# A two-layer graph, state-space and LSTM kernel: first loads, a pool over the set-up's memory, and the place of the recurrence's weight preparation

## The chip, the cores and the metric

The kernel runs on one core of a Trainium2 chip. The metric is device time in microseconds (us) of one execution. The engines are named as the profile names them: PE (matrix multiply, with PEld for its weight loads), DVE (vector), ACT (scalar and activation functions), POOL (GpSimd), SP (the engine that issues most DMAs; its instruction queue is SPq).

## The reference, cut to what matters

The input is x of shape (32, 512, 256) and an integer adjacency adj of shape (32, 512, 512). The 32 entries of the first axis are called elements here. Two layers follow each other, each with a residual connection around each of its two halves:

```python
x = x + L0_gnn(layernorm(x), adj, ...)   # per-element graph attention with edge types, 4 heads
x = x + L0_ffn(layernorm(x), ...)        # per-element Mamba-2 block, 512 tokens in chunks
x = x + L1_gnn(layernorm(x), adj, ...)   # per-element graph attention, one head
x = x + L1_ffn(layernorm(x), ...)        # LSTM over the 512 tokens, all 32 elements at once
```

The first three steps work on one element at a time. The fourth is an LSTM of 512 dependent time steps whose batch is the 32 elements. It needs all elements of the third step before its first time step. Its weights (`wih`, `whh`, the biases, `wl`, `bl`, `fw`, `bw`) are used there alone.

## The kernel before, in words

`layers_per_batch` does the first three steps for all elements and writes the result to the DRAM tensor `X3`; `recurrence` does the LSTM from `X3`. A second copy of `layers_per_batch` in a conditional block stands for adjacencies of other values and is not taken in these runs.

**Set-up (lines 105 to 247).** Constants are made, then some twenty weights are loaded through SP's queue in the order in which the lines stand: `w0`, `w0t`, `asrc`, `adst`, three rows, `win` (1160 KB), and so on to `a1`. Weights that only the set-up uses (`w0t`, `asrc`, `adst`, `normw`, `woutt`, `wlin`, `w1t`, `a1`) lie in the pool `wset`. PE multiplies some of them together (L154, L166, L243), DVE copies the results out (L205, L212, L247). Then `setup.close()` (L249) gives the memory of `wset` back, and the pools `io`, `one` and `two`, opened after it, may take it. `io` holds the element inputs: `adj` (1024 KB, one buffer) and `x` (512 KB, four buffers).

**One element.** `plain0` (L470) loads `adj` and `x` (L474, L476), normalises x, makes a transposed 8-bit adjacency, and computes the attention of layer 0. `after0` (L315) adds it to x after a normalisation per head, with POOL for the reciprocal root (L54, L56) and for the last products and sums (L336, L337). `mamba_in` (L582) normalises again and transposes (xm, mT), `mamba_dt` (L593) makes step sizes and decays, `mamba` (L665) does the rest in 25 steps; the first thing in it that the profile shows on ACT is the Silu of L680, and POOL does `ce` (L729), `xdd` (L776) and the gating of `xh` (L800) in it. `plain1` (L910) is the attention of layer 1, and `after1` (L853) stores the element to `X3` (L862). Mamba's tiles `csr`, `ce`, `bT`, `cT` and `ssr` have one buffer each, in the pool `one`.

**What sets the order of the work.** The parts of all elements are written as Python generators that are merged by a hand-made clock (L988 to L1001): `mamba` of element b runs from b to b+1, `plain0` of element b+2 from b+0.86 to b+1.54, `after0` from b+1.65 to b+1.76, `plain1` of element b-1 from b+0.571 to b+0.86. This gives the program order. From it the framework fixes, at build time, one order of instructions for each engine: an instruction goes in front of others that stand ahead of it in the program if its inputs are ready earlier by the framework's own time estimates. Each engine then works through its order and waits at each instruction for its inputs. `recurrence` has a hand-written order instead (L1255).

**The recurrence's weights.** `recurrence_weights` (L1030) is one more generator, which brings the LSTM's weights into another order and scale and stores them to the DRAM tensor `wr`. Its place on the clock is 3.25 plus 0.375 for each step (L996). It begins with a head: `wl`, `bl` and two biases are loaded and combined, then `fw` and `bw` are loaded, halved and stored. Then come 16 items, 8 of `wih` and 8 of `whh`. An item loads raw columns (L1099 and L1101, or four loads at L1105), subtracts (L1108), reorders and scales with a memset and four products into the tile `rwt` (L1051, L1057), and stores `rwt` to `wr` (L1116). `rwt` has one buffer, so the memset of the next item waits until the store of the item before has landed. The rows stored are 128, but 127 (`r = P - 1`, L1115) for the last four items of `wih`. In the trace all of this stands between 17.7 and about 159 us: none of its inputs depend on anything, so it was put in front of what stands ahead of it in the program. `recurrence` loads `wr` at L1259.

Of the kernel before, what the change touches and what calls it, by code (L numbers as in the profile page):

```python
# [19 lines left out]
P = 128  # L20
N = 512
# [54 lines left out]
def layers_per_batch(ctx, tc, c, a, X3, odd=None, wr=None):  # L76
# [22 lines left out]
    def load_row(src, name):  # L99
        t = wp.tile([P, src.shape[1]], F32, name=name)  # L100
        nc.sync.dma_start(out=t, in_=src.to_broadcast([P, src.shape[1]]))
        return t


    tri = wp.tile([P, P], F32, name="tri")
    late = wp.tile([P, P], F32, name="late")
# [14 lines left out]

    setup = ExitStack()
    wset = setup.enter_context(tc.tile_pool(name="wset", bufs=1))
    w0 = load_k(a.w0, D, "w0")
    w0t = load_k(a.w0t, D, "w0t", wset)
    asrc = load_k(a.asrc, T0, "asrc", wset)
    adst = load_k(a.adst, T0, "adst", wset)
    bias0 = load_row(a.bias0, "bias0")
    gamma = load_row(a.gamma, "gamma")
    beta = load_row(a.beta, "beta")  # L130
    win = load_k(a.win, DIN, "win")
    convw = load_k(a.convw, 4, "convw")
    convb = load_k(a.convb, 1, "convb")
    dtb = wp.tile([NH, 1], F32, name="dtb")
    nc.sync.dma_start(out=dtb, in_=a.dtb.rearrange("o h -> h o"))
    alog = load_row(a.alog, "alog")
    dcol = load_k(a.dcol, 1, "dcol")
    normw = load_k(a.normw, 1, "normw", wset)
    woutt = load_k(a.woutt, DI, "woutt", wset)
    wlin = load_k(a.wlin, D, "wlin", wset)  # L140
    blin = load_row(a.blin, "blin")
    w1 = load_k(a.w1, D, "w1")
    w1t = load_k(a.w1t, D, "w1t", wset)
    a1 = load_k(a.a1, 2, "a1", wset)

    def score_weights0(vec, half, name):

# [99 lines left out]
        nc.vector.tensor_scalar(wc[:, cc, :], pw[:, :D], normw[:, cc, :], None, ALU.mult)  # L247

    setup.close()  # L249
    io = ctx.enter_context(tc.tile_pool(name="io", bufs=2))  # L250
    one = ctx.enter_context(tc.tile_pool(name="one", bufs=1))
    two = ctx.enter_context(tc.tile_pool(name="two", bufs=2))

# [86 lines left out]
    def attention0(b, state):  # L340


        adj = io.tile([P, NT, N], I32, tag="adj", bufs=1, name=f"adj{b}")
        nc.sync.dma_start(out=adj, in_=a.adj[b].rearrange("(i p) j -> p i j", p=P))
        x = io.tile([P, NT, D], F32, tag="x", bufs=4, name=f"x{b}")
        nc.sync.dma_start(out=x, in_=a.x[b].rearrange("(i p) d -> p i d", p=P))
        xn = two.tile([P, NT, D], F32, tag="rowa", name=f"xn{b}")
        layernorm(nc, small, c, xn, x, NT)
        nc.gpsimd.tensor_tensor(x, x, beta.unsqueeze(1).to_broadcast([P, NT, D]), ALU.add)
# [120 lines left out]
    def plain0(b, state):  # L470


        adj = io.tile([P, NT, N], I32, tag="adj", bufs=1, name=f"adj{b}")
        nc.sync.dma_start(out=adj, in_=a.adj[b].rearrange("(i p) j -> p i j", p=P))  # L474
        x = io.tile([P, NT, D], F32, tag="x", bufs=4, name=f"x{b}")
        nc.sync.dma_start(out=x, in_=a.x[b].rearrange("(i p) d -> p i d", p=P))  # L476
        xn = two.tile([P, NT, D], F32, tag="rowa", name=f"xn{b}")
        layernorm(nc, small, c, xn, x, NT)
        nc.gpsimd.tensor_tensor(x, x, beta.unsqueeze(1).to_broadcast([P, NT, D]), ALU.add)
# [113 lines left out]
    def mamba_dt(b, state):  # L593

        mT = state["mT"]

        csr = one.tile([P, N], F32, tag="csr", name=f"csr{b}")
        dtr = csr[64 : 64 + NH, :]
        pd = bank(f"pdt{b}")
        for k in range(DK):  # L600
            nc.tensor.matmul(pd[:NH], win[:, k, DIN - NH :], mT[:, k, :], start=(k == 0), stop=(k == DK - 1))
        nc.scalar.activation(dtr, pd[:NH], AF.Identity, bias=dtb)

        def columns(rows, at, name):

            pt = bank(f"p{name}")
            for i in range(NT):
                nc.tensor.transpose(pt[:, i * NH : (i + 1) * NH], rows[:, i * P : (i + 1) * P], at)
            t = small.tile([P, NT, NH], F32, tag=name[:3], name=name)
            nc.vector.tensor_copy(t.rearrange("p i h -> p (i h)"), pt[:, : NT * NH])  # L610
            return t

        raw = columns(dtr, c.ident[64 : 64 + NH, 64 : 64 + NH], f"raw{b}")
        yield


        ee = small.tile([P, NT, NH], F32, tag="ee", name=f"ee{b}")
        nc.vector.scalar_tensor_tensor(ee, raw, -1.0, raw, ALU.mult, ALU.min)
        nc.scalar.activation(ee, ee, AF.Exp)
        u = small.tile([P, NT, NH], F32, tag="u", name=f"u{b}")  # L620
        nc.vector.tensor_scalar(u, ee, 2.0, None, ALU.add)
        nc.vector.reciprocal(u, u)
        nc.vector.tensor_tensor(u, u, ee, ALU.mult)
        u2 = small.tile([P, NT, NH], F32, tag="u2", name=f"u2{b}")
        nc.vector.tensor_tensor(u2, u, u, ALU.mult)
        q = small.tile([P, NT, NH], F32, tag="q", name=f"q{b}")
        nc.vector.tensor_scalar(q, u2, 2.0 / 17, None, ALU.mult)
        for m in (15, 13, 11, 9, 7, 5, 3):
            nc.vector.scalar_tensor_tensor(q, q, 2.0 / m, u2, ALU.add, ALU.mult)
        nc.vector.scalar_tensor_tensor(q, q, 2.0, u, ALU.add, ALU.mult)  # L630
        dt = small.tile([P, NT, NH], F32, tag="dt", name=f"dt{b}")
        nc.vector.scalar_tensor_tensor(dt, raw, 0.0, q, ALU.max, ALU.add)
        nc.vector.tensor_tensor(da[:, :, :NH], dt, aneg.unsqueeze(1).to_broadcast([P, NT, NH]), ALU.mult)
        yield


        pcs = bank(f"pcs{b}")
        for i in range(NT):
            nc.tensor.matmul(pcs[:32, i * P : (i + 1) * P], da[:, i, :], tri, start=True, stop=True)
        nc.scalar.copy(csr[:NH, :], pcs[:NH])  # L640
        nc.scalar.activation(csr[32 : 32 + NH, :], pcs[:NH], AF.Exp)
        line = way.tile([1, 2 * NH * N], F32, tag="line", name=f"line{b}")
        for n in range(2):
            nc.scalar.dma_start(
                out=line[:, n * NH * N : (n + 1) * NH * N].rearrange("o (h l) -> (o h) l", h=NH),
                in_=csr[32 * n : 32 * n + NH, :],
            )
        cs = columns(csr[:NH, :], c.ident[:NH, :NH], f"cs_{b}")
        pdc = bank(f"pdc{b}")
        nc.tensor.matmul(pdc[:, : NT * NH], late, da[:, :, :NH], start=True, stop=True)  # L650
        nc.tensor.matmul(pdc[:, NT * NH : 2 * NT * NH], ones, da[:, :, :NH], start=True, stop=True)
        dec = small.tile([P, 2, NT, NH], F32, tag="dec", name=f"dec{b}")
        nc.scalar.activation(dec.rearrange("p a i h -> p (a i h)"), pdc[:, : 2 * NT * NH], AF.Exp)
        yield

        ce = one.tile([P, NC, N - P], F32, tag="ce", name=f"ce{b}")
        for k in range(2):
            nc.sync.dma_start(
                out=ce[k * DS : (k + 1) * DS],
                in_=line[:, NH * N :].rearrange("o (c two l) -> o c two l", two=2, l=N)[:, :, k, P:].to_broadcast([DS, NC, N - P]),  # L660
            )
        state.update(dt=dt, cs=cs, dec=dec, ce=ce, line=line)
        yield

    def mamba(b, state):  # L665
# [14 lines left out]
            nc.scalar.activation(zs[:, cc, :], pz, AF.Silu)  # L680
            yield
        xh = two.tile([P, NC, N], F32, tag="wide", bufs=4 if odd is not None else 3, name=f"xh{b}")
        bT = one.tile([DS, N], F32, tag="bT", name=f"bT{b}")
        cT = one.tile([P, N], F32, tag="cT", name=f"cT{b}")
        def convolved(cc):
            pz = channels(DI + cc * P, f"px{b}_{cc}")
            acc = two.tile([P, N], F32, tag="acc", name=f"acc{b}_{cc}")
# [147 lines left out]
        pss = bank(f"pss{b}")  # L835
        for cc in range(NC):
            nc.tensor.matmul(pss[32 * cc : 32 * (cc + 1), :], ones[:, :32], zs[:, cc, :], start=True, stop=True)
        ssr = one.tile([P, N], F32, tag="ssr", name=f"ssr{b}")
        nc.scalar.copy(ssr, pss)
        pst = bank(f"psc{b}")  # L840
        for i in range(NT):
# [151 lines left out]
    ]  # L993
    if odd is not None:
        rw = ctx.enter_context(tc.tile_pool(name="rw0", bufs=1))
        streams.append(3.25 + (nb - 8) / 64 * n for n, _ in enumerate(recurrence_weights(nc, rw, a, wr)))  # L996
    END = nb + 10
    at = [next(t) for t in streams]
    while min(at) < END:
# [27 lines left out]
        nc.vector.tensor_scalar(odd, pf[:1, :1], P - 0.5, None, ALU.is_lt)  # L1027


def recurrence_weights(nc, pool, a, wr):  # L1030

# [15 lines left out]
    def ordered(raw, n, s):  # L1049
# [7 lines left out]
            nc.gpsimd.tensor_scalar(dst, src, half[g] * s, None, ALU.mult)  # L1057
        return t


    wl = tile_(P, 2 * DK, "rwl")
    for q in range(Q):
        for l in range(2):
            nc.sync.dma_start(
# [2 lines left out]
            )  # L1067
    yield
    nc.gpsimd.tensor_tensor(wl[:, :DK], wl[:, DK:], wl[:, :DK], ALU.subtract)
    bl = tile_(P, 2, "rbl")  # L1070
    nc.sync.dma_start(out=bl, in_=a.bl.to_broadcast([P, 2]))
    b = [tile_(P, 4 * J, f"rwraw{n}") for n in range(2)]
    for t, src in zip(b, (a.bih, a.bhh)):
        nc.sync.dma_start(out=t[:Q], in_=src.rearrange("o (q r) -> (o q) r", q=Q))
    yield
# [6 lines left out]
    nc.sync.dma_start(out=last, in_=t[:Q])  # L1082
    yield
    for n, src in enumerate((a.fw, a.bw)):
        t = tile_(P, W, "rwt")
        for q in range(Q):
            nc.sync.dma_start(out=t[q * GB : (q + 1) * GB, :J], in_=src[q : q + 1, :].to_broadcast([GB, J]))
        yield
        nc.gpsimd.tensor_scalar(t[:, :J], t[:, :J], 0.5, None, ALU.mult)
        yield  # L1090
        nc.sync.dma_start(out=wr[:, n0 + n * J : n0 + (n + 1) * J], in_=t[:, :J])
        yield
    for n, (src, s) in enumerate(((a.wih, 1.0), (a.whh, 0.5))):
        for k in range(DK):
            for q in range(Q):
                raw = tile_(P, 4 * J, f"rwraw{q % 2}")
                cols = slice(q * 4 * J, (q + 1) * 4 * J)
                if n == 0:
                    nc.sync.dma_start(out=raw, in_=src[k * P : (k + 1) * P, cols])  # L1099
                    off = tile_(P, 4 * J, "rwoff")  # L1100
                    nc.sync.dma_start(out=off, in_=src[D - 1 : D, cols].to_broadcast([P, 4 * J]))  # L1101
                else:
                    for r in range(Q):
# [352 lines left out]
```

## Time and profile before

| What | us |
|---|---|
| median of 3 runs (lowest, highest) | 4697.27 (4695.42, 4697.93) |
| the profiled execution's own time | 4702.24 |
| its span, first to last instruction | 4700.4 |
| first `adj` load issued (L474) | 29.9 |
| first Silu of `mamba`, element 0 (L680) | 146.3 |
| store of element 0 and of element 31 to `X3` issued (L862) | 334.9 and 3380.2 |
| first load of the recurrence issued (L1161) | 3386.4 |
| busy: PE, DVE, ACT, POOL | 3892.5, 3388.8, 2926.4, 1332.6 |

A row of the timeline gives the start and length of a group of instructions in us, the engine, the line of the kernel, the operation with the tile that it writes and those that it reads, their shape, the number of instructions, and in brackets how long the engine had been idle before it and what ended that. A row of the waits gives the waiting engine, tile and line, what it waited for, and total us, times and longest us. POOL's busy time ends in the 29th of the 40 slices of the page: the recurrence hardly uses it.

### The profile page before, as it was taken

What the parts mean: (1) busy time and instruction counts of PE and PEld (TensorE: products, weight loads), DVE (VectorE), ACT (ScalarE), POOL (GpSimd) and SP (SyncE); (2) the same over time, 40 slices, a digit from 0 to 9 for tenths busy, and PEclk for the clock granted to TensorE, in tenths of its full rate; (3) what the DMA queues carried; (4) which work ended last, traced back from release to release, by engine and by line L of the source; (5) the groups of instructions that cost most, each with busy time, mean ns of one, the idle gap of its engine ahead of it and who ended that gap; (6) DMA issues with size and microseconds to landing.
All of it is one profiled execution on the core that took longest, in us unless ns stands there. A gap on an engine that the chain in (4) does not pass through costs nothing. (4 is left out here: it accounts for less than half of the span.)

```text
span 4700.4 us, 115757 instructions
## 1 busy us (share of the span) xinstructions
PE 3892.5 (83%) x46798; PEld 2418.6 (51%) x46798; DVE 3388.8 (72%) x10205; ACT 2926.4 (62%) x6724; POOL 1332.6 (28%) x1148
## 2 busy tenths in 40 slices
PE   3788888888888888888888888888688888888883
PEld 2344444444444544444444444444466666666662
DVE  3466676666666666666666676666489999999997
ACT  2577777777777777776677776766444444444442
POOL 3433333433333433333433333432100000000000
PEclk7899999999999999999999999999799999999997
DMA  4222111222111222111122211211212222222225
GB/s 114 60 64 71 59 59 57 64 73 71 59 59 57 64 73 71 59 59 57 58 70 70 64 62 57 63 51 50 63 35 44 44 44 46 46 47 44 44 42 164
DMA packets 273754, 288.69 MB, mean 61 GB/s; under 512 B 151872, under 2 KB 224536, under 8 KB 271032
## 3 DMA queue, kind: packets, MB, share of 16 engines
q1 hardware_dynamic: 269832, 271.32, 20.3%
q10 hardware_dynamic: 3216, 9.81, 0.7%
q8 instruction: 372, 6.09, 0.5%
q14 instruction: 174, 1.43, 0.1%
q0 software_dynamic: 160, 0.04, 0.0%
HBM read 227.09 MB, written 37.11 MB: 56 GB/s over the span
## 5 line engine op out<-in xcount | busy, mean ns | idle before, releaser
L1243 PE MATMUL pg<-wall,h 128*32 128x96 f32 x16352 | 559.2, 277 | 176.7 <-DVE h L1325 169.3
L1243 PEld LDWEIGHTS pg<-wall,h 128*32 128x32 f32 x16352 | 374.8, 109 | 350.3 <-DVE h L1325 331.8
L1243 PE MATMUL pg<-wall,xTr 128*32 128x96 f32 (+1 forms) x16384 | 549.0, 274 | 0.0
L467 DVE SCALAR_TENSOR_TENSOR w<-w,adjT 128x1024 f32<-128x1024 f32 x256 | 348.1, 1380 | 247.6 <-ACT w L461 247.6
L1243 PEld LDWEIGHTS pg<-wall,xTr 128*32 128x32 f32 x16384 | 447.7, 110 | 4.9 <-issue 0.3
L743 ACT ACTIVATE g<-bc,cs 128x128 f32<-128x128 f32 x1024 | 321.9, 391 | 137.3 <-PE py L811 137.3
L1302 ACT ACTIVATE z<-pg 128x96 f32<-128x96 f32 x512 | 128.7, 251 | 439.3 <-PE pg L1243 439.3
L693 DVE SCALAR_TENSOR_TENSOR acc<-px,convw,acc 128x511 f32<-128x511 f32 (+2 forms) x480 | 347.2, 745 | 75.8 <-ACT acc L688 68.0
L461 ACT ACTIVATE w<-rb,neg,colsa 128x512 f32<-128x512 f32 x512 | 387.4, 806 | 9.9 <-DMA rb<-linea 6.0
L729 POOL TENSOR_TENSOR ce<-ce,cT 128x384 f32<-128x384 f32 x128 | 185.2, 1477 | 667.7 <-ACT cT L701 650.5
L533 PE MATMUL pav<-w,hb 128*64 128x512 f32 x1024 | 352.5, 615 | 22.5 <-DVE w L467 22.5
L830 PE MATMUL po<-wc,xh 128*128 128x256 f32 x1024 | 283.4, 422 | 100.2 <-POOL xh L800 100.2
L1313 ACT ACTIVATE z<-z 128x32 f32<-128x32 f32 x1024 | 234.7, 229 | 168.0 <-DVE z L1311 100.8
L945 PE MATMUL pov<-wb,wv 128*128 128x257 f32 x1024 | 243.1, 390 | 89.3 <-DVE wv L467 89.3
L54 POOL TENSOR_SCALAR ve<-mv 128x4 f32<-128x4 f32 x32 | 6.2, 195 | 1064.1 <-DVE mv L1167 1064.1
L672 PE MATMUL px<-mT,win 128*128 128x512 f32 x640 | 305.2, 607 | 0.0
L830 PEld LDWEIGHTS po<-wc,xh 128*128 128x128 f32 x1024 | 203.2, 213 | 145.3 <-POOL xh L800 115.6
L945 PEld LDWEIGHTS pov<-wb,wv 128*128 128x128 f32 x1024 | 191.5, 192 | 133.1 <-DVE wv L467 105.3
L56 POOL TENSOR_TENSOR rs<-ve,mhalf 128x4 f32<-128x4 f32 (+1 forms) x192 | 255.2, 1329 | 15.9
L800 POOL TENSOR_TENSOR xh<-xh,zs 128x512 f32<-128x512 f32 x128 | 175.5, 1381 | 282.1 <-DVE xh L799 282.1
L1325 DVE STREAM_TRANSPOSE h<-hh 128x32 f32<-128x32 f32 x1024 | 216.7, 212 | 34.9
L672 PE MATMUL pz<-mT,win 128*128 128x512 f32 x512 | 240.4, 602 | 0.0
(243 smaller groups left out, 8492.0 us busy)
## 6 DMA issues: line engine op xcount, KB each, us to landing
bc<-line SPq DMA_DIRECT2D x128, 512.0 KB
adj<-in_adj_dram SPq DMA_DIRECT2D x32, 1024.0 KB
rb<-linea SPq DMA_DIRECT2D x64, 512.0 KB
ce<-line SPq DMA_DIRECT2D x64, 384.0 KB
x<-in_x_dram SPq DMA_DIRECT2D x32, 512.0 KB
X<-x SPq DMA_DIRECT2D x32, 512.0 KB
xt<-X SPq DMA_DIRECT2D x128, 128.0 KB
x<-X SPq DMA_DIRECT2D x128, 128.0 KB
```

The source lines that it names most:

```text
L56: nc.gpsimd.tensor_tensor(rs, ve, c.mhalf[:, :n], ALU.pow)
L461: nc.scalar.activation(w[:, t, k, :], rb[:, k, :], AF.Relu, bias=neg1, scale=cols[:, 2 * m + t, h + k : h + k + 1],)
L467: nc.vector.scalar_tensor_tensor(w[:, :, k, :], w[:, :, k, :], 1.0, edges, ALU.add, ALU.mult)
L533: nc.tensor.matmul(pa[k * HO : (k + 1) * HO, :], hb[:, j, 2 * q + k, :], w[:, t, k, :], start=(j == 0), stop=(j == NT - 1),)
L672: nc.tensor.matmul(pz, win[:, k, col : col + P], mT[:, k, :], start=(k == 0), stop=(k == DK - 1))
L693: nc.vector.scalar_tensor_tensor(acc[:, s:], pz[:, : N - s], convw[:, cc, k : k + 1], acc[:, s:], ALU.mult, ALU.add)
L743: nc.scalar.activation(g[:, i, k, :], bc[:, k, i * P : (i + 1) * P], AF.Relu, bias=cs[:, i, 2 * cc + k : 2 * cc + k + 1], scale=-1.0,)
L830: nc.tensor.matmul(po[:, i * D : (i + 1) * D], xh[:, cc, it * P : (it + 1) * P], wc[:, cc, :], start=(cc == 0), stop=(cc == NC - 1),)
L945: nc.tensor.matmul(po[:, : D + 1], ws[j // 2][:, j % 2, 0, it * P : (it + 1) * P], wb[:, j, :], start=(j == 0), stop=(j == NT - 1),)
L1243: nc.tensor.matmul(p[q * GB : (q + 1) * GB, :], lhs[k], w[:, k, q, s:e], start=(start and k == 0), stop=(stop and k == DK - 1),)
L1313: nc.scalar.activation(z[:, (10 + n) * H : (11 + n) * H], z2[:, 4 * n * H : (4 * n + 1) * H], AF.Tanh, scale=0.5)
L1325: nc.vector.transpose(h[n], half)
```

## The change

Four things are changed. (1) The pool `io` is opened ahead of the set-up, element 0's `x` is loaded ahead of everything else, and its `adj` after `w0t`, `asrc`, `adst` and `w0`; the other set-up loads are put in another order. For later elements `x` is now loaded ahead of `adj`. (2) A new pool `mam` is opened after `setup.close()` and holds `csr`, `ce`, `bT`, `cT` and `ssr`, one buffer each, in the memory that `wset` gave back. (3) `recurrence_weights` is placed at `nb - 1.75` plus 1.5/64 for each step, that is from 30.25 on. (4) Each tile that it loads from DRAM is first written in one column by a POOL copy from x of the element that the clock has reached (`begun`), so that the loads can't be issued ahead of that x.

```diff
+    io = ctx.enter_context(tc.tile_pool(name="io", bufs=2))
+
+    def load_x(b):
+        x = io.tile([P, NT, D], F32, tag="x", bufs=4, name=f"x{b}")
+        nc.sync.dma_start(out=x, in_=a.x[b].rearrange("(i p) d -> p i d", p=P))
+        return x
+
+    def load_adj(b):
+        adj = io.tile([P, NT, N], I32, tag="adj", bufs=1, name=f"adj{b}")
+        nc.sync.dma_start(out=adj, in_=a.adj[b].rearrange("(i p) j -> p i j", p=P))
+        return adj
+
+    x0 = load_x(0)
...
-    w0 = load_k(a.w0, D, "w0")
     w0t = load_k(a.w0t, D, "w0t", wset)
     asrc = load_k(a.asrc, T0, "asrc", wset)
     adst = load_k(a.adst, T0, "adst", wset)
+    w0 = load_k(a.w0, D, "w0")
+    adj0 = load_adj(0)
+    beta = load_row(a.beta, "beta")
     bias0 = load_row(a.bias0, "bias0")
     gamma = load_row(a.gamma, "gamma")
-    beta = load_row(a.beta, "beta")
+    alog = load_row(a.alog, "alog")
+    blin = load_row(a.blin, "blin")
     win = load_k(a.win, DIN, "win")
...
-    alog = load_row(a.alog, "alog")
     dcol = load_k(a.dcol, 1, "dcol")
+    w1t = load_k(a.w1t, D, "w1t", wset)
+    a1 = load_k(a.a1, 2, "a1", wset)
+    w1 = load_k(a.w1, D, "w1")
     normw = load_k(a.normw, 1, "normw", wset)
     woutt = load_k(a.woutt, DI, "woutt", wset)
     wlin = load_k(a.wlin, D, "wlin", wset)
-    blin = load_row(a.blin, "blin")
-    w1 = load_k(a.w1, D, "w1")
-    w1t = load_k(a.w1t, D, "w1t", wset)
-    a1 = load_k(a.a1, 2, "a1", wset)
...
     setup.close()
-    io = ctx.enter_context(tc.tile_pool(name="io", bufs=2))
+
+    mam = ctx.enter_context(tc.tile_pool(name="mam", bufs=1))
     one = ctx.enter_context(tc.tile_pool(name="one", bufs=1))
...
-        adj = io.tile([P, NT, N], I32, tag="adj", bufs=1, name=f"adj{b}")
-        nc.sync.dma_start(out=adj, in_=a.adj[b].rearrange("(i p) j -> p i j", p=P))
-        x = io.tile([P, NT, D], F32, tag="x", bufs=4, name=f"x{b}")
-        nc.sync.dma_start(out=x, in_=a.x[b].rearrange("(i p) d -> p i d", p=P))
+        x, adj = (load_x(b), load_adj(b)) if b else (x0, adj0)
...
-        csr = one.tile([P, N], F32, tag="csr", name=f"csr{b}")
+        csr = mam.tile([P, N], F32, tag="csr", name=f"csr{b}")
...
-        streams.append(3.25 + (nb - 8) / 64 * n for n, _ in enumerate(recurrence_weights(nc, rw, a, wr)))
+        now = lambda: states[int(min(at))]["x"][:, 0, 0:1]
+        streams.append(nb - 1.75 + 1.5 / 64 * n for n, _ in enumerate(recurrence_weights(nc, rw, a, wr, now)))
...
+    def begun(t, *columns):
+        for n in columns or (0,):
+            nc.gpsimd.tensor_copy(t[:, n : n + 1], now())
+        return t
+
+    yield
+
-    wl = tile_(P, 2 * DK, "rwl")
+    wl = begun(tile_(P, 2 * DK, "rwl"), 0, DK)
...
-    bl = tile_(P, 2, "rbl")
+    bl = begun(tile_(P, 2, "rbl"))
...
-    b = [tile_(P, 4 * J, f"rwraw{n}") for n in range(2)]
+    b = [begun(tile_(P, 4 * J, f"rwraw{n}")) for n in range(2)]
...
-        t = tile_(P, W, "rwt")
+        t = begun(tile_(P, W, "rwt"))
...
-                raw = tile_(P, 4 * J, f"rwraw{q % 2}")
+                raw = begun(tile_(P, 4 * J, f"rwraw{q % 2}"))
...
-                    off = tile_(P, 4 * J, "rwoff")
+                    off = begun(tile_(P, 4 * J, "rwoff"))
```

The tiles `ce`, `bT`, `cT` and `ssr` change their pool as `csr` does.

More of the change, by code (lines that the diff above doesn't have):

```diff
@@ L470, in plain0 @@
     def plain0(b, state):
[L473 to L476, printed above, removed]
+        x, adj = (load_x(b), load_adj(b)) if b else (x0, adj0)
         xn = two.tile([P, NT, D], F32, tag="rowa", name=f"xn{b}")
@@ L654, in mamba_dt @@
         yield
-        ce = one.tile([P, NC, N - P], F32, tag="ce", name=f"ce{b}")
+        ce = mam.tile([P, NC, N - P], F32, tag="ce", name=f"ce{b}")
         for k in range(2):
@@ L682, in mamba @@
         xh = two.tile([P, NC, N], F32, tag="wide", bufs=4 if odd is not None else 3, name=f"xh{b}")
-        bT = one.tile([DS, N], F32, tag="bT", name=f"bT{b}")
-        cT = one.tile([P, N], F32, tag="cT", name=f"cT{b}")
+        bT = mam.tile([DS, N], F32, tag="bT", name=f"bT{b}")
+        cT = mam.tile([P, N], F32, tag="cT", name=f"cT{b}")
         def convolved(cc):
@@ L837, in mamba @@
             nc.tensor.matmul(pss[32 * cc : 32 * (cc + 1), :], ones[:, :32], zs[:, cc, :], start=True, stop=True)
-        ssr = one.tile([P, N], F32, tag="ssr", name=f"ssr{b}")
+        ssr = mam.tile([P, N], F32, tag="ssr", name=f"ssr{b}")
         nc.scalar.copy(ssr, pss)
@@ L1027, in layers_per_batch, with recurrence_weights @@
         nc.vector.tensor_scalar(odd, pf[:1, :1], P - 0.5, None, ALU.is_lt)
-def recurrence_weights(nc, pool, a, wr):
+def recurrence_weights(nc, pool, a, wr, now):
     Q, J = 4, 64
```

## The prediction

> **What bounds the kernel now.** I first read the page's 40 slices for the stages, then one marker per element, then the timeline of the first 150 us, the waits in it, and POOL's timeline near the end. The first Silu of `mamba` (L680) starts at 146.3 us in element 0 and at 3279.4 in element 31: 31 steps of 101.07. The first load of the recurrence is at 3386.4, the end at 4700.4. So the span is a ramp of 146.3, a pace of 31 × 101.07 = 3133.1, a drain of 107.0 and a recurrence of 1314.0. The change has no line in the recurrence. Its parts lie in the ramp and just ahead of the drain, and both are chains: what is late there moves everything behind it.
>
> The ramp's first stall, from the timeline of the first us:
>
> ```profile
> 29.41 0.48 DVE L247 TENSOR_SCALAR wc<-pwc,normw 128x256 f32<-128x256 f32 x1 [0.38 <-PE pwc L243]
> 29.92 0.38 SPq L474 DMA_DIRECT2D adj<-in_adj_dram  x1
> 30.35 2.03 SPq L476 DMA_DIRECT2D x<-in_x_dram  x3
> 35.65 1.23 DVE L481 TENSOR_SCALAR msk<-adj 128x2048 bf16<-128x2048 int32 x1 [5.76 <-DMA adj<-in_adj_dram]
> 37.00 0.75 DVE L65 BATCH_NORM_STATS2 bnst<-x 128x6 f32<-128x256 f32 x2
> ```
>
> The reader is to see that element 0's inputs are issued the moment that the last set-up product has been copied out (29.89): `io` takes the set-up's memory. The second stall, from the waits between 78 and 130 us and then the timeline there (DVE's and POOL's rows):
>
> ```profile
> ACT rowsa L433 <- issue: 32.6, 1, 32.6
> DVE o L335 <- POOL rs L56: 23.3, 1, 23.3
> POOL rwt L1051 <- DMA wr<-rwt: 23.0, 5, 7.5
> ```
>
> ```profile
> 90.95 1.22 DVE L333 TENSOR_REDUCE vs<-sq 128x16 f32<-128x1024 f32 x1 [1.18 <-ACT sq L331]
> ...
> 101.12 0.10 POOL L1051 MEMSET rwt<- 128x2 f32 x1 [7.46 <-DMA wr<-rwt]
> ...
> 110.68 0.10 POOL L1051 MEMSET rwt<- 128x2 f32 x1 [7.44 <-DMA wr<-rwt]
> ...
> 112.18 0.21 POOL L54 TENSOR_SCALAR ve<-vs 128x16 f32<-128x16 f32 x1
> ```
>
> `after0`'s variance is ready at 92.17, but POOL does L54 only at 112.18: in its order stand two memsets of `rwt`, each behind a store of `wr` that takes 8.1 us to land (102.58 to 110.68). DVE and ACT stand still meanwhile.
>
> **Part 1, first loads: -26 us.** `w0` and `w0t`, 512 KB issued from 0.79, were in use at 4.75. x has 512 KB and is now first, so I put it at 4.8 instead of 37.0: 32.2 earlier at best. `adj` has 1.54 MB ahead of and in itself after x; at the 276 GB/s seen between 30 and 40 us that is 5.6 us more, at the 99 of the first 10 us 15.6. It lands between 10.4 and 20.4, and its first use on the path (L467, 57.02 before) is 20 us after x, so it mostly hides. Two things take from the 32.2. The row `rb` (L448, issued at 50.52, which would be 18.3) stands on SP behind the set-up loads, whose issue lasted to 17.69 with three long issues (2.86, 2.84, 2.02); two more and 1.5 MB in front of them make it 18.6 to 25, so 0 to 7 lost. And PE's 1.84 + 5.58 us of set-up products (L166, L243) now come from the loads issued last, and may stand in PE's order ahead of layer 0's products: 0 to 7. I take 6 for the two together; bounds -18 and -32.
>
> **Part 2, the ramp without the weight preparation: -28.8 us.** What POOL started late because of it, each from rows of its timeline: `o` plus bias, ready 80.09, started 83.44: 3.35. L54 as above: 20.01. L337, L336 ended 121.21, started 121.89: 0.68. `mamba_in`'s L54, ready 126.68, started 127.66: 0.98, and L56 after it, 127.86 to 128.59: 0.73. Together 25.75; they are in series. On SP, element 1's `rb` was issued at 139.73, behind a store at 139.28, though its line was written from 129.97 on; ACT idled 5.78 for it just ahead of the Silu. I take 3 of 0 to 5.8. Bounds for the part: -20 (L54's stall alone) and -31.5. With the stalls gone the next in the ramp is its own chain of normalisations, products and DMA round trips, which stays.
>
> **Part 3, the same work from 30.25 on: +14 us.** The work itself: an item of `wih` has 0.10 + 1.36 + 0.73, one of `whh` 0.10 + 1.36 + 0.22; with 8 of each and 31 copies at 0.19 (the nearest row, POOL L1076, 128x1) and 4.3 for the head it is 41 us of POOL, and 87 DMA issues on SP of 0.3 to 0.6. POOL is 28% busy, so length is not the question; the waits are. `begun` needs x after L588, which ends at 3160.1 for element 30 and 3262.2 for element 31. By the clock the head and the eight `wih` items take element 30's x, the `whh` items element 31's. As the work was put in front by up to four elements before, I expect it right behind L588. In the rows the head costs about 27 us (five round trips of 2 to 3 and its products; an estimate), four items 4.1 each (stores at 64.39, 69.13, 73.26, 76.81), the 127-row ones 9.6 (101.12 to 110.68): 82 us, plus what POOL does between, so to about 3250.
>
> What POOL does between is on the chain there:
>
> ```profile
> 3198.76 5.85 POOL L729 TENSOR_TENSOR ce<-ce,cT 128x384 f32<-128x384 f32 x4 [24.03 <-ACT cT L701]
> 3219.29 2.35 POOL L578 TENSOR_TENSOR o<-o,bias 128x1024 f32<-128x1024 f32 x1 [14.68 <-DVE o L571]
> 3221.60 4.37 POOL L776 TENSOR_TENSOR xdd<-xdt,dec 128x512 f32<-128x512 f32 x3
> ...
> 3222.70 1.12 PE L783 MATMUL pst<-xdd,bn 128*128 128x512 f32 x2 [1.39 <-POOL xdd L776]
> ```
>
> PE waits for `xdd` at once, and behind it on PE stand the rest of `mamba(30)` and of `plain1(29)`. In the ramp the framework put the POOL work of three items (the 6th to 8th) between `o` plus bias and L54, where the chain itself had 9 us; so it orders as if an item took some 3 us, and the four 127-row ones take 6 more than that. POOL can fall 4 × 6 = 24 us behind its order, as far as idle time (24.0 ahead of `ce`, 14.7 ahead of `o`) hasn't absorbed it. PE has 9.8 idle of 40 us between 3220 and 3260 to make good. 24 - 10 = 14. The `whh` items (4 to 5 each, done by about 3300) meet a drain in which POOL idles 17.1 ahead of `ce` and 13.8 ahead of `xdd`; SP's `bc` and `ce` loads (3283 to 3288) may stand up to 6 behind them. Bounds: 0, and 24 + 6 = 30. The new write-after-read wait (L848 of `mamba` must not overwrite x before the copies) has 20 us at 3270 and 40 after 3300; the load of `wr` at 3389 has 85.
>
> A row and a rule speak to the 8.1 us. Between 103 and 112 us the DMA view gives:
>
> ```profile
> GB/s 0 9 9 14 23 18 14 77 78 78 82 96 96 110 78 37 23 18 23 18 23 23 18 23 18 23 18 23 18 23 18 23 14 0 0 0 0 0 0 0
> ```
>
> The store's tail runs at 18 to 23 GB/s with nothing else in the queue, where 128-row stores landed in 2.0 to 2.2 us. The Trainium skill ("DMA: Bandwidth & Descriptors", Why a DMA increments its semaphore by 16 and not by 1) says that a DMA from SP runs on the largest number of engines up to 16 that divides its outer dimension, so on one for 127 rows. By that rule the slow stores move along with the change and speak against it, and the sum is the one here; if they were only the ramp's crowding, part 3 would be 0 and the time 14 lower.
>
> **Part 4, the pools and the order of x and `adj`: 0.** `mam` holds the same tiles with the same single buffers; its first use (`csr`, 136.37) comes 106 us after the last set-up read. In the pace, `adj` and `x` are issued as their buffers come free, 11 us apart (3050.91, 3061.98), whichever stands first. That the framework orders the 31 equal steps a little differently can't be read from the trace; stores to `X3` are 99.2 or 102.2 apart, and I allow 0.3 per step either way: ±9.
>
> **Sum.** 4702.24 (the profiled execution) - 26 - 28.8 + 14 = 4661.5. The median of the runs is 4.97 below the profiled execution, so 4656.
>
> **Rivals.**
> - Part 3 is free: POOL's idle time takes it all, since 38.7 us of it lie ahead of `ce` and `o` alone. Against it stands the ramp, where the same rows cost 25. 4642 or less. Chance 0.15.
> - Start and preparation both pay less: the loads queue up (part 1 at -18, part 2 at -23) and POOL's lag is all on the path (+24): 4680; 4667 to 4682. For it speaks the 99 GB/s of the first 10 us. Chance 0.15.
> - The end waits for the weights: if the work isn't put in front but starts so late that `wr` is complete only after element 31, L1259 waits, and the time grows. From its first load to its last store it took 139 us before (17.7 to 157.0). Then it must have started by 3247 (old clock) to be hidden; a start after 3302 costs more than parts 1 and 2 bring, and at 3340, the last place the clock allows, the result is 4697 - 55 + 93 = 4735. Against it: x is ready at 3160 and 3262. Chance 0.06.
> - The ramp isn't what sets the end: the pace takes the gain back (by 55 / 31 = 1.8 per step) because element 0 now runs against more of element 1's work. 4697, within the ±0.2% that a measurement of this kernel can tell from no change (±9.4 us). Against it: step 0 to 1 of the Silu was 101.0, like all. Chance 0.04.
>
> The forecast, 4642 to 4667, has 0.60. The range reaches from 4632 (part 1 at -32, part 3 at 0) to 4682. Faster by over 0.2%: 0.60 + 0.15 + 0.15 = 0.90; the same 0.04; slower 0.06.
>
> **What would show it.** Right: x's first issue below 1 us and its L65 by 5 to 8; no `rwt` memset before 3000; L54 of `after0(0)` within 1 us of DVE's `vs`; the first Silu at 86 to 98; POOL idle behind `wr` stores between some 3100 and 3260, shifted by 55, four times about 8 us, and the step from the 30th to the 31st Silu longer than 103.4. Wrong: a first Silu later than 105, a pace off 101.07 by over 0.3, or L1259 waiting for a store of `wr`.

## The result, and the profile after

The changed kernel took 4685.39 us (median of 8 runs, 4683.61 to 4689.60), the kernel before 4699.36 (8 runs beside them, 4695.42 to 4707.27): a ratio of 0.9972, 95% interval 0.9962 to 0.9982. It is faster by about 14 us. The forecast was 41 us, a median of 4656 in a range of 4642 to 4667, and the time lies above that. The profiled execution of after took 4689.60, its span 4687.4; that of before, 4702.24 and 4700.4.

Cut at the stores to `X3` and at the first load of the recurrence, the two spans differ so (us; first Silu of element 0, then the store of each element):

| Stretch | before | after | difference | forecast |
|---|---|---|---|---|
| start to first Silu | 146.3 | 99.7 | -46.6 | |
| start to store of element 28 | 3161.2 | 3106.9 | -54.3 | -54.8 |
| element 28 to 29 | 102.1 | 130.0 | +27.9 | |
| element 29 to 30 | 72.1 | 86.7 | +14.6 | |
| element 30 to 31, and on to the recurrence's first load | 51.0 | 50.8 | -0.2 | |
| the last three together | 225.2 | 267.5 | +42.3 | +14 |
| recurrence | 1314.0 | 1313.0 | -1.0 | 0 |

So the start gave what was forecast, and the end took three times as much. The pages of the profile show the same in their 40 slices of 117 us, first before, then after:

```profile
PE   3788888888888888888888888888688888888883
POOL 3433333433333433333433333432100000000000
```

```profile
PE   6888888888888888888888888885588888888883
POOL 2333433333433333433333443354100000000000
```

The reader is to see the first digit of PE, 3 before and 6 after, and the pair of fives in slices 28 and 29 (3164 to 3398 us): the stretch in which PE still has `mamba` to do. POOL's 5 and 4 in slices 27 and 28 are the moved work.

The start in the timeline of after: the first load, its use, the first weights' row `w` of layer 0, and POOL's L54 of `after0` with the variance that it waits for.

```profile
0.80 0.46 SPq L108 DMA_DIRECT2D x<-in_x_dram  x1
...
4.79 0.75 DVE L65 BATCH_NORM_STATS2 bnst<-x 128x6 f32<-128x256 f32 x2 [3.69 <-DMA x<-in_x_dram]
...
11.54 1.28 ACT L494 ACT_TABLE_LOAD   x1 [11.54 <-DMA adj<-in_adj_dram]
12.84 2.00 ACT L494 ACTIVATE sqa<-adj,neghalf 128x2048 bf16<-128x2048 int32 x1
...
16.21 2.06 ACT L71 ACTIVATE xn<-x,off,rs 128x256 f32<-128x256 f32 x4
...
34.65 0.81 ACT L475 ACTIVATE w<-rb,neg,colsa 128x512 f32<-128x512 f32 x1
```

```profile
70.77 1.22 DVE L350 TENSOR_REDUCE vs<-sq 128x16 f32<-128x1024 f32 x1 [1.18 <-ACT sq L348]
72.07 0.21 POOL L54 TENSOR_SCALAR ve<-vs 128x16 f32<-128x16 f32 x1 [6.47 <-DVE vs L350]
```

x is in use at 4.79 instead of 37.0, but the first `w` comes only 20.1 us earlier (34.65 against 54.77). ACT has the adjacency's `sqa` and its table load ahead of the normalised x (L71) in its order, and waits for `adj` until 11.54; so x stands until 16.21. The prediction had taken `adj` as mostly hidden. L54 starts 0.1 us after its variance; before it stood 20 us.

The end in the waits of after, between 3100 and 3345 us (waiting engine, tile and line; what it waited for; total, times, longest), and in POOL's timeline:

```profile
POOL rwt L1063 <- DMA wr<-rwt: 46.0, 12, 8.1
...
PE pst L794 <- POOL xdd L787: 29.1, 1, 29.1
DVE o L336 <- POOL o L589: 26.6, 1, 26.6
...
ACT dec L664 <- DMA wr<-rwt: 7.1, 1, 7.1
```

```profile
3163.01 0.18 POOL L1074 COPY rwraw<-x 128x1 f32<-128x1 f32 x1
3171.03 0.10 POOL L1063 MEMSET rwt<- 128x2 f32 x1 [7.84 <-DMA wr<-rwt]
...
3181.65 0.10 POOL L1063 MEMSET rwt<- 128x2 f32 x1 [8.01 <-DMA wr<-rwt]
...
3192.24 0.10 POOL L1063 MEMSET rwt<- 128x2 f32 x1 [8.10 <-DMA wr<-rwt]
3192.30 2.34 POOL L589 TENSOR_TENSOR o<-o,bias 128x1024 f32<-128x1024 f32 x1
3194.59 4.02 POOL L787 TENSOR_TENSOR xdd<-xdt,dec 128x512 f32<-128x512 f32 x3
```

Three 127-row stores stand in POOL's order ahead of the `o` plus bias (L589) that layer 0 of the last element needs and ahead of the `xdd` (L787) that `mamba(30)` needs. PE does nothing worth naming in that time. The windows view from 3166 to 3193 us (length, then busy us and instructions of PE, PEld, DVE, ACT and POOL, the granted clock, the DMA share, GB/s):

```profile
3166.00:3193.00 27.00, 0.63 (x5) 0.39 (x4) 1.81 (x3) 2.73 (x4) 5.24 (x15) 0.58 0.14 45
```

Every engine is nearly idle, POOL too (5.24 busy of 27): it waits for stores.

### The profile page after: what moved, and what is told of

It is laid out like the page before. It is cut to its first block, busy times and chain, and to the rows that moved or that the text cites. A ratio compares the mean times of both kernels' runs of the same rounds, so it can differ in the third digit from the quotient of the medians.

```text
span 4687.4 us, 115801 instructions
## 1 busy us (share of the span) xinstructions
PE 3891.0 (83%) x46798; PEld 2415.0 (52%) x46798; DVE 3387.5 (72%) x10205; ACT 2927.1 (62%) x6724; POOL 1336.9 (29%) x1179
## 5 line engine op out<-in xcount | busy, mean ns | idle before, releaser
L54 POOL TENSOR_SCALAR ve<-mv 128x4 f32<-128x4 f32 x32 | 6.2, 194 | 1061.5 <-DVE mv L1185 1061.5
```

## The experiments

My theory: the end's 42 us come from the moved preparation, most of it from the four 127-row stores, behind which POOL, in its order, holds back `o` and `xdd`. A first rival: they come from SP, whose queue now has the preparation's 87 issues among the element loads. A second: they have nothing to do with the preparation, but with the new order of `x` and `adj` and the pools.

In the table, each ratio is to runs of before made beside that kernel (their medians 4697.3 to 4699.4); the last four columns are from the profiled executions: first Silu, store of element 28, the steps 28 to 29 and 29 to 30, and the end (store of element 28 to the recurrence's first load).

| Kernel | median us | ratio to before [95%] | Silu(0) | X(28) | steps | end |
|---|---|---|---|---|---|---|
| before | 4699.4 | 1 | 146.3 | 3161.2 | 102.1, 72.1 | 225.2 |
| after | 4685.4 | 0.9972 [0.9962, 0.9982] | 99.7 | 3106.9 | 130.0, 86.7 | 267.5 |
| e1 loads only | 4681.9 | 0.9964 [0.9951, 0.9976] | 109.1 | 3148.6 | 102.1, 72.2 | 225.6 |
| e2 weights only | 4705.5 | 1.0017 [1.0007, 1.0026] | 117.6 | 3127.5 | 130.0, 87.1 | 267.8 |
| e3 split | 4662.3 | 0.9920 [0.9903, 0.9938] | 101.6 | 3105.2 | 113.5, 79.7 | 245.4 |
| e4 more 127 | 4704.8 | 1.0008 [0.9999, 1.0018] | 100.4 | 3107.4 | 149.7, 86.5 | 289.1 |
| e5 spread | 4705.8 | 1.0016 [1.0006, 1.0026] | 98.2 | 3158.8 | 102.1, 72.2 | 225.5 |
| e6 spread, split | 4698.4 | 1.0000 [0.9990, 1.0011] | 100.5 | 3178.0 | 102.1, 72.1 | 225.6 |
| e7 before, split | 4669.9 | 0.9936 [0.9920, 0.9953] | 122.6 | 3135.3 | 102.1, 72.1 | 225.7 |
| e8 no pool `mam` | 4691.4 | 0.9990 [0.9981, 1.0000] | 105.7 | 3108.3 | 130.3, 86.8 | 268.3 |
| e9 loads, split | 4662.0 | 0.9922 [0.9908, 0.9935] | 108.6 | 3120.3 | 102.1, 72.2 | 225.9 |
| e10 last, split | 4656.3 | 0.9908 [0.9892, 0.9923] | 99.1 | 3101.5 | 103.1, 89.6 | 241.5 |

**e1_loads_only**: after, with the preparation at its old place on the clock and without the copies of `begun`.

```diff
-        streams.append(nb - 1.75 + 1.5 / 64 * n for n, _ in enumerate(recurrence_weights(nc, rw, a, wr, now)))
+        streams.append(3.25 + (nb - 8) / 64 * n for n, _ in enumerate(recurrence_weights(nc, rw, a, wr, now)))
...
-        for n in columns or (0,):
-            nc.gpsimd.tensor_copy(t[:, n : n + 1], now())
-
-    yield
```

> The changed kernel with the weight preparation back at its old place (3.25 plus 0.375 per step) and without the copies from x; the loads and the pool mam stay. My theory, that the ramp's two stalls pay separately and that the whole loss is at the end: the start gains 20 to 26 us, POOL's stall in after0 of element 0 stays at some 20, and the end costs nothing: 4699 - 20 to 26 = 4673 to 4679, with the step from the 30th to the 31st Silu back at about 103. Rival, that the earlier loads only move the wait to the weight preparation, which now runs into element 0's chain: below 10 us of gain, 4690 or more.

The end is 225.6, as before: the second rival falls, with the new pools and a new order of `x` and `adj` in this kernel. The first Silu comes 37.2 us earlier than before, yet the store of element 28 only 12.6, and the median gains 17 us, less than the 20 to 26 expected. The stall in `after0` of element 0, expected to stay at some 20, is gone (its variance ends at 75.46, L54 starts at 75.54): the slow stores now hit later work. The waits of e1 between 40 and 140 us:

```profile
POOL rwt L1063 <- DMA wr<-rwt: 26.0, 5, 8.8
...
ACT dec L664 <- DMA line<-csr: 18.0, 1, 18.0
```

The step from the first Silu to the next element's took 126.4 in e1, against 101.0 before.

**e2_weights_only**: before, with the moved preparation alone.

```diff
-        streams.append(3.25 + (nb - 8) / 64 * n for n, _ in enumerate(recurrence_weights(nc, rw, a, wr)))
+        now = lambda: states[int(min(at))]["x"][:, 0, 0:1]
+        streams.append(nb - 1.75 + 1.5 / 64 * n for n, _ in enumerate(recurrence_weights(nc, rw, a, wr, now)))
...
+            nc.gpsimd.tensor_copy(t[:, n : n + 1], now())
```

> The kernel before with the weight preparation alone moved to 30.25 and begun by copies from x; the loads and pools as before. My theory: the ramp loses about 27 to 29 us of stalls, the end takes 42 as in the changed kernel: slower by 13 to 15, 4712 to 4714, and the start of element 0's loads stays at about 30 us. Rival, that the 42 at the end come from the new pools or the new order of the loads: then the end costs less than 20 here and the time falls to 4690 or lower.

The move alone is a small loss, 6 us in the median where 13 to 15 were expected: 33.7 us won by element 28, 42.6 lost at the end, nearly the 42.3 of after without any of its loads. The waits of e2 in its last elements:

```profile
DVE o L319 <- POOL o L578: 26.9, 1, 26.9
```

**e3_split**: after, with each 127-row store as two, of 112 and 15 rows. Same data, four more issues on SP.

```diff
-                nc.sync.dma_start(out=wr[:r, o0 : o0 + W], in_=t[:r])
+                for s0, s1 in ((0, P),) if r == P else ((0, 112), (112, r)):
+                    nc.sync.dma_start(out=wr[s0:s1, o0 : o0 + W], in_=t[s0:s1])
```

> The changed kernel with each 127-row store of wr as two, of 112 and 15 rows. My theory, that POOL's order is held up by the landing of the 127-row stores and PE stands behind POOL's xdd: an item takes about 4 instead of 9.6 us, the bias on o starts some 24 us earlier, PE's wait for xdd falls from 29 to below 8, the fourth store's wait (6.9) falls too: 25 to 32 us faster than the changed kernel, 4653 to 4660. Rival, that SP's queue (87 issues, here 4 more) or the sheer POOL work holds the chain: within 5 us of the changed kernel, 4680 to 4690.

23 us faster than after, just short of the 25 to 32 expected, and 22 of it at the end (267.5 to 245.4). The 8 us waits are gone; POOL's timeline and the waits of e3:

```profile
3170.43 0.10 POOL L1063 MEMSET rwt<- 128x2 f32 x1 [2.02 <-DMA wr<-rwt]
```

```profile
DVE o L336 <- POOL o L589: 10.5, 1, 10.5
```

**e4_more_127**: after, with the stores of the first four `wih` items as 127 rows and 1 row, so that eight stores are slow.

```diff
-                nc.sync.dma_start(out=wr[:r, o0 : o0 + W], in_=t[:r])
+                cuts = (0, P - 1, P) if n == 0 and k == 0 else (0, r)
+                for s0, s1 in zip(cuts, cuts[1:]):
+                    nc.sync.dma_start(out=wr[s0:s1, o0 : o0 + W], in_=t[s0:s1])
```

> The changed kernel with the first four items of wih also stored by a DMA of 127 rows, and one more of the last row. My theory: four more items of 9.6 instead of 4 us; each adds about 6 to POOL's lag in front of o's bias, less what idle time is left ahead of ce (8.6): 14 to 24 us slower than the changed kernel, 4699 to 4710, and PE's wait for xdd grows from 29 by about as much. Rival, that the end's loss is SP's queue or POOL's work: four more issues of 0.3 to 0.4 us and nothing else, 4685 to 4690.

19 us slower than after. With 0, 4 and 8 slow stores (e3, after, e4) the end takes 245.4, 267.5 and 289.1, so each slow store costs 5.5 of the 6 us that it lasts longer. e3 and e4 both have four more issues on SP than after and go opposite ways: for the slow stores' part, the rival on SP falls. For the 20 us that e3 leaves no run separates SP's loads and stores from POOL's order. In the waits of e4 the lines of `xdd` and `o` have grown by some 16 us:

```profile
POOL rwt L1063 <- DMA wr<-rwt: 65.4, 14, 8.1
...
PE pst L794 <- POOL xdd L787: 45.4, 1, 45.4
DVE o L336 <- POOL o L589: 43.0, 1, 43.0
```

What e3 leaves is as telling: with no slow store the end still takes 20 us more than before.

**e5_spread** and **e6_spread_split**: after with the preparation spread over elements 3 to 27 at one step per 0.375, with `begun` to keep it there; e6 has the split of e3 as well. The idea was that one item per element goes into POOL's idle time behind L599.

```diff
-        streams.append(nb - 1.75 + 1.5 / 64 * n for n, _ in enumerate(recurrence_weights(nc, rw, a, wr, now)))
+        streams.append(3.25 + (nb - 8) / 64 * n for n, _ in enumerate(recurrence_weights(nc, rw, a, wr, now)))
```

> The changed kernel with the weight preparation begun by copies from x as there, but at the old places 3.25 plus 0.375 per step, so that about one item is begun in each element from the 3rd to the 25th. My theory, that the loss is several 127-row stores one behind another in front of POOL's bias on o: here each stands alone right behind L599 of its element, where POOL then idles over 20 us, so nearly nothing is lost: the ramp keeps its 54, the end costs 0 to 5, the elements with a 127-row store 0 to 3 each: 4640 to 4658. Rival, that the work costs what it costs wherever it runs beside a full element (42 us in all): 4680 to 4690.

> As e5, and with the 127-row stores as 112 and 15 rows. My theory: as one such store alone is hidden, the split gives nothing more: within 5 us of e5, 4640 to 4655. Rival, that each 127-row store also holds up other transfers in the steady elements: 10 to 25 us faster than e5.

That idea fell. The start (98.2) and the end (225.5) are both good in e5, and the time is lost between: the steps of the Silu are 97 to 101 up to element 6 and 105 to 106.5 in each of the next eight. POOL's timeline of e5, in one of them:

```profile
892.10 0.18 POOL L1074 COPY rwoff<-x 128x1 f32<-128x1 f32 x1
896.28 0.73 POOL L1126 TENSOR_TENSOR rwraw<-rwraw,rwoff 128x256 f32<-128x256 f32 x1 [4.00 <-DMA rwoff<-in_wih_dram]
896.97 2.36 POOL L490 TENSOR_TENSOR x<-x,beta 128x1024 f32<-128x1024 f32 x1
899.28 1.37 POOL L1069 TENSOR_SCALAR rwt<-rwraw 128x64 f32<-128x64 f32 x4
900.73 0.19 POOL L54 TENSOR_SCALAR ve<-ssc 128x4 f32<-128x4 f32 x1
```

The item waits 4.00 us for its own load, with the chain's L54 behind it. DVE's wait for that root was 5.6 there, against 1.4 in an undisturbed element. In these eight steps PE's granted clock was 0.94 to 0.97, against 0.98 in the two before them, and PE was busy 88.7 to 91.0 us a step instead of 85.6 to 87.2; whether that follows from the waits or is a second cause was not separated. Slow stores are not the cause, since e6 has none and is no better off than before; its store of element 28 is from the highest of its ten runs (4719), so only its median is used.

**e7_before_split**: before, with the split of e3 and nothing else.

> The kernel before with the 127-row stores alone split into 112 and 15 rows. My theory, that POOL's stall of 20 us in after0 of element 0 was three such stores: it falls to 2 to 6, and the time by 14 to 20: 4679 to 4685. Rival, that the stall in the ramp was the number of items or SP's queue: within 5 of before, 4694 or more.

27 us faster than before, from two lines, where 14 to 20 were expected. The first Silu comes 23.7 earlier, the store of element 28 25.9. L54 of `after0` starts 1.0 us after its variance, where it stood 20:

```profile
91.92 1.22 DVE L333 TENSOR_REDUCE vs<-sq 128x16 f32<-128x1024 f32 x1 [1.18 <-ACT sq L331]
...
94.13 0.21 POOL L54 TENSOR_SCALAR ve<-vs 128x16 f32<-128x16 f32 x1
```

**e8_no_mam**: after, with `csr`, `ce`, `bT`, `cT` and `ssr` in the pool `one` as before.

```diff
-    mam = ctx.enter_context(tc.tile_pool(name="mam", bufs=1))
...
-        csr = mam.tile([P, N], F32, tag="csr", name=f"csr{b}")
+        csr = one.tile([P, N], F32, tag="csr", name=f"csr{b}")
```

> The changed kernel without the pool mam: csr, ce, bT, cT and ssr lie in the pool one again, so that one takes the set-up's memory, and its first tiles (msk, xT) with it. My prediction put the pool at 0; if that holds by itself, 4685 as the changed kernel. My theory now: xT or msk must wait until the set-up's products are read, at about 33 us instead of 18.8 for xT, so 8 to 15 us slower than the changed kernel, 4693 to 4700: the pool is what lets the early loads pay.

6 us slower than after in the first Silu as in the median, less than the 8 to 15 expected; the intervals of the two ratios just meet. Without `mam`, ACT's waits up to 50 us begin with this:

```profile
ACT xT L281 <- DVE wc L263: 14.2, 1, 14.2
```

The transposed x of element 0 takes memory that the set-up still uses, and is copied at 33.78 instead of 18.84. With `mam` on that memory first, `xT` lies elsewhere and needn't wait. Of these 15 us, 6 reach the first Silu; what covers the other 9 is open.

**e9_loads_split**: e1 with the split of e3.

> As e1 (early loads and mam, weight preparation at its old place and not begun by copies), with the 127-row stores split into 112 and 15 rows. My theory, that the 127-row stores are what makes the preparation dear wherever it stands: the step from Silu 0 to Silu 1, 126 in e1, falls to 97 to 103, and the time by 20 to 28 from e1's 0.9964: ratio 0.990 to 0.9925, about 4653 to 4663, level with the changed kernel with the split (0.992). Rival, that in the ramp the preparation costs by its number of POOL operations and DMAs: under 10 us faster than e1, ratio 0.994 or more.

The loss in e1's first step is nearly gone (102.8 instead of 126.4), and the preparation at its old place costs nothing at the end. It is as fast as e3: 0.9922 and 0.9920.

**e10_last_split**: e3 with the preparation placed a little later.

```diff
-        streams.append(nb - 1.75 + 1.5 / 64 * n for n, _ in enumerate(recurrence_weights(nc, rw, a, wr, now)))
+        streams.append(nb - 1 + 0.75 / 64 * n for n, _ in enumerate(recurrence_weights(nc, rw, a, wr, now)))
```

> The changed kernel with the split stores and the preparation placed at 31.0 plus 0.75/64 per step, so that all of it takes the last element's x and stands in the drain, where POOL has 17.1 us idle ahead of ce and 13.8 ahead of xdd. My theory: in the changed kernel with the split the end still costs 20 us (o plus bias 10.5 late, the rest in the drain); here the first part goes and the drain takes 8 to 20: ratio 0.989 to 0.992. Rival, that the drain is all chain and each item's wait of POOL stands in it: 16 items and the head cost 25 to 45, ratio 0.993 to 0.9975.

The lowest median of all, 0.9908. The step 28 to 29 is 103.1 again, the step 29 to 30 89.6, and the end costs 16 us more than before instead of 42. The waits of e10 there:

```profile
PEld pst L794 <- POOL xdd L787: 12.9, 5, 7.9
```

It beats both kernels. That it beats e9 (4656.3 against 4662.0) is not certain, since their intervals overlap.

## Why the prediction was wrong

- **Parts 1 and 2 together: right, in part by luck.** -54.8 forecast, -54.3 measured at element 28. The split between the two is less good, and its errors cancel. The first `w` moved 20.1, not 26; e1 bears out that the loads alone can't bring the sum, because the slow stores then fall on element 1. e2 puts part 2 at 33.7 by element 28, and -54.3 + 33.7 leaves 20.6 for part 1. Both are near the bounds given (18 to 32; 20 to 31.5), part 2 above its own. The first Silu at 99.7 is 1.7 past the stretch named; the other 8 us appear by the store of element 28.
- **The signs named for the start: right.** x issued at 0.80 and used at 4.79; L54 at 72.07. No `rwt` memset of an item before 3133, and no wait for `wr` in the recurrence (last store issued at 3294.53, first load at 3377.2).
- **The place of the moved work and its four waits: right, the lag's size by luck.** The waits are 7.84, 8.01, 8.10 and 6.93 us, and DVE waited 26.6 us for `o` plus bias where a lag of 24 was forecast. But the 24 was four slow stores at 6, and only three stand ahead of `o`; they make 16.1 of the 26.6 (in e3 it was 10.5), and the items themselves, counted as hidden, make the other 10.5.
- **Part 3's size: wrong. This is the step that failed.** "24 - 10 = 14" let PE make good 10 of the lag from its idle time between 3220 and 3260. It made good nothing. PE was busy 0.63 of 27 us while it waited, the step grew by 27.9, the whole lag, and afterwards PE had as much idle time as ever. The windows of the 40 us from 2.7 us ahead of PE's first `pst`, before and then after:

```profile
3220.00:3260.00 40.00, 30.20 (x165) 21.65 (x164) 28.15 (x52) 21.40 (x42) 22.90 (x15) 0.91 0.07 20
```

```profile
3192.99:3232.99 40.00, 27.91 (x158) 19.59 (x159) 25.84 (x48) 18.09 (x36) 22.91 (x15) 0.88 0.03 7
```

PE's idle time, 9.8 us before, is 12.1 after: PE waits there for the same chain (in after 4.2 for POOL's `xh`, 2.9 for DVE's `wv`, 2.1 for ACT's `rowsv`), which is itself late. It isn't a reserve. e4 confirms it: each further slow store is paid at 5.4 of 6.

- **The same term, its bound: wrong too.** "24 + 6 = 30" took an item of normal length to be hidden, and charged only the excess of the four slow ones. e3 has no slow store and still costs 20.2 at the end. Of after's 42.3, then, 22.1 are the slow stores and 20.2 is the preparation itself in this place. In e3 some of that can be seen: `o` is 10.5 late, PE waits 13.0 once ahead of `pst` (1.39 before), and in after as in e3 L54 of the next normalisation stands 3.5 behind an item's `rwoff`. The step 28 to 29 takes 11.4 of the 20.2, about the lag of `o`; the 7.6 of the next step and the last 1.2 can't be put to single lines.
- **The whh items: 0 to 6 expected; the step in which they run grew by 14.6.** In that step, 29 to 30, the last `wih` item runs too, and with it the fourth 127-row store, issued at 3250.08. ACT is held there as well as POOL. It writes the second half of the rows for `line` until 3258.64, and their two DMAs are issued only from 3262.97 on:

```profile
3250.08 0.25 SPq L1134 DMA_DIRECT2D wr<-rwt  x1
...
3256.18 0.56 ACT L651 COPY csr<-pcs 8x512 f32<-8x512 f32 x1
...
3258.05 0.59 ACT L652 ACTIVATE csr<-pcs 8x512 f32<-8x512 f32 x1
3258.12 0.10 POOL L1063 MEMSET rwt<- 128x2 f32 x1 [6.93 <-DMA wr<-rwt]
...
3262.97 2.70 ACTq L655 DMA_DIRECT2D line<-csr  x2
...
3265.72 0.22 ACT L664 ACTIVATE dec<-pdc 128x64 f32<-128x64 f32 x1 [7.09 <-DMA wr<-rwt]
```

In e3 the first of them follows the copy by 0.13 us, `dec` waited 0.35, and the step grew by 7.6. The wait at `dec` is 7.09 to 7.14 in all four runs with a 127-row store at this place (after, e2, e4, e8) and 0.35 in the two with it split (e3, e10), so it goes with the slow store. By what path is open: the store was in flight when the first of the two DMAs was due (3256.9), but it had landed at 3258.1, 4.9 us before that DMA was issued. How the remaining 7.6 divides between the last `wih` item and the `whh` items is open too.

- **Part 4: not nothing.** The pool is worth 6 us (e8). The forecast looked at the first use of mamba's tiles, when the question was who would lie on the set-up's memory in their place.
- **The rivals.** The kernel's time is near the second (4680), but not by its way: the start paid in full. The first, part 3 free, is the opposite of what was found. Pace (100.86 per element between the stores of 0 and 28, 100.94 before) and the recurrence (1313.0 after, 1314.0 before) spoke against the other two.
- **A sum.** The low end of the range, 4632 for part 1 at -32 and part 3 at 0, comes to 4636 by its own terms; nothing hangs on it.
- **The rule on the 127 rows held.** The Trainium skill ("DMA: Bandwidth & Descriptors", Why a DMA increments its semaphore by 16 and not by 1) has a DMA run on the largest divisor of its outer dimension up to 16, by which 127 rows go on one engine, 112 on 16 and 15 on 15. The runs agree in time, some 2 us for the split store against 8.1; the number of engines itself no view here shows.

## What to carry to other kernels

Work that is moved out of a crowded start has to go where its engine's order isn't on the chain: a low busy share (POOL 29%) says nothing of that, and in this kernel the waits inside the moved work were paid nearly in full (5.4 to 5.5 of 6 us a slow store) by what stood behind them in the same order. Idle time of another engine behind such a wait made nothing good (PE, 9.8 us before and 12.1 after), so it can't be counted as a reserve; count a lag as recovered only by an engine that has independent work ready then. And before moving a slow transfer, look at why it is slow: the two-line split brought more on the kernel before (27 us, e7) than the whole change (14).

## What the runs showed of the hardware

A 127-row store of `rwt` lands some 8.1 us after its issue in after, one of 128 rows, or of 112 and 15, after some 2. In after, the DMA view from 3164 to 3172 us shows the store that lands at 3171.0: its tail runs at 21 GB/s, with nothing else left to move.

```profile
GB/s 5 26 21 15 15 21 97 113 123 87 87 159 138 282 277 62 31 21 21 21 21 21 21 21 21 21 21 21 21 21 21 21 20 26 26 10 0 0 0 0
```

Not expected was the second effect: with such a store on SP's side shortly before, the issue of a DMA on ACT's queue stood too (7.09 us of ACT, 0.35 with the store split). e1's wait of 18.0 for `line` may be of the same kind: there the DMAs were due at 114.9 and issued at 134.15, after slow stores issued at 103.59, 116.16 and 125.73. The cause is open in both.
